# Paired logits in one PSUM tile and a second top-p search cut into eight steps

## The chip, the cores and the metric

The kernel runs on one core of one Trainium2 chip. The metric is the device time of one execution in microseconds (us), lower is better. The engines of the core work side by side and each takes its instructions in program order: TensorE (PE, matmuls and transposes; its weight loads are PEld in the profile), VectorE (DVE), ScalarE (ACT), GpSimd (POOL) and the DMA queue of SyncE (SP). Matmul results land in PSUM, whose tiles are handed out from pools with a fixed number of buffers.

## The reference, cut to what matters

The network has four layers over 3327 nodes with 256 features. The change touches the last layer only. It does two steps of a diffusion by a given matrix `S` and of an attention whose weights are cut to the most probable 90% of each row:

```python
def _top_p_attention(X, W1, W2, W3):
    q = X @ W1.T @ W2.T
    k = X @ W3.T
    logits = q @ k.T / TAU
    probs = jax.nn.softmax(logits, axis=-1)
    idx = jnp.argsort(-probs, axis=-1)
    sp = jnp.take_along_axis(probs, idx, axis=-1)
    cs = jnp.cumsum(sp, axis=-1)
    keep_sorted = cs - sp < TOP_P                 # TOP_P = 0.9
    mask = ...                                    # the kept places of each row
    A = probs * mask
    return A / jnp.maximum(A.sum(-1, keepdims=True), 1e-12)

R = (S + I) / row sums
Xf = Xa = X
for n in range(2):
    A = _top_p_attention(Xa, W1, W2, W3)
    Xf = R @ Xf                                   # diffusion
    Xa = A @ Xa                                   # attention
    Z = Z + Xf @ U1[n].T + Xa @ U2[n].T
h = X + Z                                         # then layer norms
```

`W1` to `W3` have 64 rows, so a logit is a product over 64 numbers. All arithmetic is fp32.

## The kernel before

The nodes are padded to 3328, which makes 26 tiles of 128 rows (`nt = 26`, `npad = 3328`). A tile of logits `e` is 128 x 3328. Queries and keys lie twice on the partitions, at 0 to 63 and at 64 to 127, so the left and the right half of a row of logits come from two matmuls over 64 partitions each (`half = 1664`, in chunks of `KC = 416`):

```python
def scores(work, psum, p, q, e):
    for c0 in range(0, half, KC):
        for h in (0, DA):                          # DA = 64
            c = c0 + (half if h else 0)
            w = min(KC, n - c)
            pl = psum.tile([P, 512], F32, name="sc")          # two buffers
            nc.tensor.matmul(pl[:, :w], q[h:h + DA, :], kT[p][h:h + DA, c0:c0 + w], start=True, stop=True)
            nc.scalar.copy(e[:, c:c + w], pl[:, :w])
        yield
```

The diffusion of a tile is 26 matmuls of 128x256 (`diffused`, line L721 in the profile). The attention of a tile transposes `e` in 26 blocks of 128x128 through PSUM tiles of four blocks each, ACT copies them to SBUF, and 26 matmuls follow (`attended`, lines L749, L751 and L753; two PSUM buffers `tp`, three SBUF buffers `wt`).

The first attention finds the threshold of a row with `search_short` (Exp on ACT, 26 Max8 over segments of 128 columns, six rounds of Max8 and MatchReplace, and one pass that keeps what lies above). The second has flatter rows and takes `search_long`, which guesses a threshold twice before it ranks the candidates:

```python
def search_long(work, sm, e, total, v, kept):
    nc.vector.max(m8, e[:, :KC])                                            # L815
    ...
    nc.scalar.activation(junk, e, AF.Exp, ..., accum_out=root)              # L819
    nc.scalar.activation(e, e, AF.Exp, bias=neg, accum_out=total)           # L820
    yield
    ...                                                                     # c1 from total and root
    nc.scalar.activation(junk, e, AF.Sign, bias=c1, scale=-1.0, accum_out=sg)                  # L829
    z = work.tile([P, npad], F32, name="z", bufs=1)
    nc.vector.scalar_tensor_tensor(z, e, c1, e, op0=ALU.is_ge, op1=ALU.mult, accum_out=m1)     # L831
    nc.vector.tensor_scalar(k1, sg, -0.5, npad / 2, op0=ALU.mult, op1=ALU.add)
    ...                                                                     # c2 from k1, m1
    nc.scalar.activation(junk, e, AF.Relu, bias=nc2, accum_out=f2)          # L849
    nc.scalar.activation(junk, e, AF.Sign, bias=c2, scale=-1.0, accum_out=sg)                  # L850
    ...
    yield
    nc.vector.tensor_scalar(k2, sg, -0.5, npad / 2, op0=ALU.mult, op1=ALU.add)                 # L863
    ...                                                                     # c3 from k2, f2
    nc.vector.scalar_tensor_tensor(z, e, c3, e, op0=ALU.is_lt, op1=ALU.mult, accum_out=rest)   # L875
    cand = segment_tops(work, z)                                            # 26 Max8, L761
    top = ranked(work, cand, RPT)                                           # L770, L772
    cs = crossing(work, v, top, base, lim)
    ...                                                                     # ties
    for r, c in ((r, half), (up, 0)):
        ...
        nc.vector.match_replace(back, drop, back, 0.0)                      # L894
    nc.vector.scalar_tensor_tensor(e, e, v, e, op0=ALU.is_ge, op1=ALU.mult, accum_out=kept)    # L895
    yield
```

Both attentions run in one loop over tiles, which works on several tiles at once so that the engines have something to do; a scheduler orders the instructions of each engine when the program is built:

```python
with ... tc.tile_pool(name="l3p", bufs=2, space=PSUM) as psum:
    for p, search, step, lead in ((0, search_short, first, (1,)), (1, search_long, second, (2, 1, 0))):
        for i in range(-lead[0], nt):
            # scores of tile i + lead[0], diffusion of a tile up to DL = 4 ahead,
            # one step of the search of each tile in lead, then:
            todo = step(work, psum, i, attended(work, psum, es[i], G if p else X), f, xfs[i])
```

`first` multiplies the result of the first attention with `U1` and `U2` and makes the keys and queries of the second (lines L913 to L929); `second` adds up and applies the layer norms (L936 to L952). `e` has three buffers, `sc`, `acc`, `tp` and `pj` two each.

Of the kernel before, what the change touches and what calls it, by code (L numbers as in the profile page):

```python
# [9 lines left out]
F32 = mybir.dt.float32  # L10
# [28 lines left out]
DL = 4  # L39
# [4 lines left out]
def gnn_kernel(ctx: ExitStack, tc: tile.TileContext, n: int, a: dict, out: bass.AP):  # L44
# [441 lines left out]
    with tc.tile_pool(name="l3", bufs=1) as pool, tc.tile_pool(name="l3d", bufs=1, space=DRAM) as dram:  # L486
# [213 lines left out]
        def scores(work, psum, p, q, e):  # L700

            if npad > n:
                nc.gpsimd.memset(e[:, n:], NEG)
            for c0 in range(0, half, KC):
                for h in (0, DA):
                    c = c0 + (half if h else 0)
                    w = min(KC, n - c)
                    pl = psum.tile([P, 512], F32, name="sc")
                    nc.tensor.matmul(pl[:, :w], q[h:h + DA, :], kT[p][h:h + DA, c0:c0 + w], start=True, stop=True)  # L709
                    nc.scalar.copy(e[:, c:c + w], pl[:, :w])  # L710
                yield
# [30 lines left out]
        def attended(work, psum, e, rhs):  # L742

            acc = psum.tile([P, D], F32, name="acc")
            for j0 in range(0, nt, 4):
                m = min(4, nt - j0)
                pt = psum.tile([P, 4, P], F32, name="tp")
# [7 lines left out]
            return acc  # L755

        def segment_tops(work, z):

            cand = work.tile([P, nseg * 8], F32, name="cand")
            for s in range(nseg):  # L760
                nc.vector.max(cand[:, s * 8:(s + 1) * 8], z[:, s * SEG:(s + 1) * SEG])  # L761
            return cand
# [30 lines left out]
        def search_short(work, sm, e, total, v, kept):  # L793


            top = ranked(work, segment_tops(work, e), RP0)
# [8 lines left out]
        def search_long(work, sm, e, total, v, kept):  # L805
# [22 lines left out]
            sg, k1, m1 = t("sg"), t("k1"), t("m1")  # L828
            nc.scalar.activation(junk, e, AF.Sign, bias=c1, scale=-1.0, accum_out=sg)  # L829
            z = work.tile([P, npad], F32, name="z", bufs=1)  # L830
            nc.vector.scalar_tensor_tensor(z, e, c1, e, op0=ALU.is_ge, op1=ALU.mult, accum_out=m1)  # L831
            nc.vector.tensor_scalar(k1, sg, -0.5, npad / 2, op0=ALU.mult, op1=ALU.add)
            rc, na = t("rc"), t("na")
# [12 lines left out]

            nc2, f2, k2, m2 = t("nc2"), t("fs2"), t("k2"), t("m2")
            nc.vector.tensor_scalar_mul(nc2, c2, -1.0)
            nc.scalar.activation(junk, e, AF.Relu, bias=nc2, accum_out=f2)  # L849
            nc.scalar.activation(junk, e, AF.Sign, bias=c2, scale=-1.0, accum_out=sg)  # L850
# [27 lines left out]
            cand = segment_tops(work, z)  # L878
            top = ranked(work, cand, RPT)
            cs = crossing(work, v, top, base, lim)  # L880

# [7 lines left out]
            for r, c in ((r, half), (up, 0)):  # L889
# [3 lines left out]
                back = e[:, c:c + half][:, ::-1]  # L893
                nc.vector.match_replace(back, drop, back, 0.0)  # L894
            nc.vector.scalar_tensor_tensor(e, e, v, e, op0=ALU.is_ge, op1=ALU.mult, accum_out=kept)  # L895
# [9 lines left out]
        def first(work, psum, it, acc, f, xf):  # L905
# [9 lines left out]
            nc.vector.tensor_copy(xt, pt)  # L915
            ps = psum.tile([P, 2, D], F32, name="pj")
            pg = psum.tile([P, 2, D], F32, name="pj")
            for k in range(4):
                nc.tensor.matmul(ps[:, 0, :], xt[:, k, :], (u1 if k < 2 else u2)[:, 0, k % 2, :],  # L919
                                 start=(k == 0), stop=(k == 3))  # L920
# [12 lines left out]
        def second(work, psum, it, acc, f, xf):  # L933
# [3 lines left out]
            yield  # L937
# [5 lines left out]
            power(rs, mv)  # L943
            nc.vector.scalar_tensor_tensor(h, h, mv[:, 0:1], g3, op0=ALU.subtract, op1=ALU.mult)
# [4 lines left out]
            power(rs, mv)  # L949
            nb = small.tile([P, 1], F32, name="nb")  # L950
# [6 lines left out]
        def unresolved(sm, psum, p):  # L957
# [14 lines left out]
            pf = psum.tile([1, nt], F32, name="pj")  # L972
# [12 lines left out]
        with tc.tile_pool(name="l3w", bufs=2) as work, tc.tile_pool(name="l3s", bufs=4) as sm, \  # L985
                tc.tile_pool(name="l3at", bufs=3) as atp, tc.tile_pool(name="l3p", bufs=2, space=PSUM) as psum:


            for p, search, step, lead in ((0, search_short, first, (1,)), (1, search_long, second, (2, 1, 0))):
                es, searches, xfs, todo = {}, {}, [], None  # L990
                for i in range(-lead[0], nt):
# [11 lines left out]
                    if p:  # L1003
                        for x in parts:
                            both(x)
# [159 lines left out]
```

## Time and profile before

| what | value |
|---|---|
| time, median of 3 (lowest, highest) | 3961.54 us (3959.18, 3976.78) |
| span of the profiled execution | 3960.8 us |
| busy: PE, DVE, ACT, POOL | 3568.0, 2724.9, 1677.1, 367.0 us |
| layers before the last one | 0 to about 2039 us |
| first attention | about 2039 to 2996 us |
| second attention | about 2996 to 3961 us |

An fp32 matmul appears as two records. The records of matmuls that follow each other overlap, so the cost of a group of them is read from where it starts to where the next one starts. In the timeline, `[0.59 <-ACT e L710]` means that the engine stood idle for 0.59 us before this group and that an ACT instruction of line L710 ended the wait. A bare `issue` is idle time for which the profile shows no wait.

### The profile page before, as it was taken

What the parts mean: (1) busy time and instruction counts of PE and PEld (TensorE: products, weight loads), DVE (VectorE), ACT (ScalarE), POOL (GpSimd) and SP (SyncE); (2) the same over time, 40 slices, a digit from 0 to 9 for tenths busy, and PEclk for the clock granted to TensorE, in tenths of its full rate; (3) what the DMA queues carried; (4) which work ended last, traced back from release to release, by engine and by line L of the source; (5) the groups of instructions that cost most, each with busy time, mean ns of one, the idle gap of its engine ahead of it and who ended that gap; (6) DMA issues with size and microseconds to landing.
All of it is one profiled execution on the core that took longest, in us unless ns stands there. A gap on an engine that the chain in (4) does not pass through costs nothing.

```text
span 3960.8 us, 41368 instructions
## 1 busy us (share of the span) xinstructions
PE 3568.0 (90%) x14863; PEld 2605.8 (66%) x14863; DVE 2724.9 (69%) x6003; ACT 1677.1 (42%) x2692; POOL 367.0 (9%) x436
## 2 busy tenths in 40 slices
PE   9999988888888877789989999999999899999975
PEld 8888754444444433378877777777777677777754
DVE  1111589999999999967743444444453999999996
ACT  0000555455555556311112333333345666666662
POOL 0000000101010101011110000000000122222210
PEclk9999999999999988889999999999999999999997
DMA  6442211111111000044422121112103122222100
GB/s 234 140 138 91 76 46 41 35 36 34 41 35 35 23 0 0 15 140 151 145 87 81 48 60 58 51 52 60 58 11 102 48 59 62 62 61 61 48 23 6
DMA packets 100530, 252.95 MB, mean 64 GB/s; under 512 B 14787, under 2 KB 49091, under 8 KB 100179
## 3 DMA queue, kind: packets, MB, share of 16 engines
q1 hardware_dynamic: 100306, 250.13, 20.7%
q8 instruction: 121, 1.98, 0.2%
q14 instruction: 103, 0.84, 0.1%
HBM read 239.86 MB, written 10.22 MB: 63 GB/s over the span
## 4 chain that ended last, share of the span: by engine, by line
PE 34%; DVE 16%; ACT 3%; issue 2%; POOL 2%; DMA 0%; POOLq 0%; ACTq 0%; DVEq 0%
PE acc L753 12%; PE acc L721 8%; PE acc L651 6%; PE sc L709 3%; DVE cand L761 3%; DVE e L894 2%; DVE e L895 2%; PE tp L749 2%; PE pj L919 1%; DVE top L770 1%; DVE z L831 1%; DVE z L875 1%; ACT junk L829 1%; DVE rest L772 1%; POOL rs L513 1%
## 5 line engine op out<-in xcount | busy, mean ns | idle before, releaser
L464 PE MATMUL y<-h,ident 128*128 128x512 f32 (+1 forms) x896 | 445.3, 644 | 72.6 <-DVE h L411 72.4
L408 DVE TENSOR_TENSOR_SCAN h<-dA,carry,db 128x512 f32<-128x512 f32 (+1 forms) x448 | 510.3, 1189 | 0.1
L761 DVE MAX8 cand<-e 128x8 f32<-128x128 f32 x676 | 143.8, 279 | 478.1 <-ACT e L710 478.1
L753 PE MATMUL acc<-G,wt 128*128 128x256 f32 x1352 | 344.3, 409 | 47.1 <-ACT wt L751 47.1
L464 PEld LDWEIGHTS y<-h,ident 128*128 128x128 f32 x896 | 188.5, 218 | 291.1 <-issue 179.6
L751 ACT COPY wt<-tp 128x512 f32<-128x512 f32 (+1 forms) x364 | 186.1, 552 | 443.0 <-PE tp L749 442.6
L753 PEld LDWEIGHTS acc<-G,wt 128*128 128x128 f32 x1352 | 269.7, 204 | 120.0 <-ACT wt L751 80.7
L239 PE MATMUL cb<-F,at 128*128 128x256 f32 x1352 | 334.0, 393 | 8.3 <-ACT m L256 8.2
L710 ACT COPY e<-sc 128x416 f32<-128x416 f32 (+1 forms) x416 | 192.5, 508 | 329.0 <-PE sc L709 329.0
L721 PE MATMUL acc<-X,at 128*128 128x256 f32 x1352 | 321.5, 388 | 2.6 <-issue 2.6
L753 PE MATMUL acc<-X,wt 128*128 128x256 f32 x1352 | 318.9, 383 | 3.0 <-ACT wt L751 2.8
L239 PEld LDWEIGHTS cb<-F,at 128*128 128x128 f32 x1352 | 261.3, 196 | 89.5 <-issue 33.5
L116 PE MATMUL acc<-xa,at 128*128 128x257 f32 x1352 | 308.4, 382 | 5.9 <-DMA at<-in_adjT 5.9
L721 PE MATMUL acc<-F,at 128*128 128x256 f32 x1352 | 308.6, 380 | 0.0
L651 PE MATMUL acc<-F,at 128*128 128x257 f32 x1352 | 303.9, 381 | 1.1 <-DVE at L648 1.1
L721 PEld LDWEIGHTS acc<-X,at 128*128 128x128 f32 x1352 | 251.7, 192 | 75.8 <-issue 44.1
L753 PEld LDWEIGHTS acc<-X,wt 128*128 128x128 f32 x1352 | 250.1, 190 | 64.2 <-ACT wt L751 33.5
L393 ACT ACTIVATE dA<-dt,A_log 128x512 f32<-128x512 f32 (+1 forms) x448 | 281.0, 681 | 12.6 <-DVE dt L370 12.2
L709 PE MATMUL sc<-kT,q 64*128 64x416 f32 x832 | 259.9, 561 | 27.5 <-ACT e L710 26.6
L116 PEld LDWEIGHTS acc<-xa,at 128*128 128x128 f32 x1352 | 255.9, 191 | 42.8 <-issue 5.9
L721 PEld LDWEIGHTS acc<-F,at 128*128 128x128 f32 x1352 | 249.6, 189 | 46.5 <-issue 13.7
L651 PEld LDWEIGHTS acc<-F,at 128*128 128x128 f32 x1352 | 253.7, 191 | 36.8 <-DVE at L648 1.4
(293 smaller groups left out, 5292.2 us busy)
## 6 DMA issues: line engine op xcount, KB each, us to landing
at<-in_adjT SPq DMA_DIRECT2D x102, 832.0 KB, 4.5
at<-in_adjT SPq DMA_DIRECT2D x156, 448.0 KB, 3.4
at<-in_adjT SPq DMA_DIRECT2D x52, 576.0 KB, 3.7
at<-in_adjT SPq DMA_DIRECT2D x52, 320.0 KB, 3.0
at<-in_adjT SPq DMA_DIRECT2D x26, 512.0 KB, 3.5
xt<-in_xT SPq DMA_DIRECT2D x26, 128.0 KB, 4.1
qd<-q SPq DMA_DIRECT2D x104, 32.0 KB, 1.9
q<-qd SPq DMA_DIRECT2D x52, 64.0 KB, 1.9
```

Source lines behind the costliest of these rows:

```text
L116: nc.tensor.matmul(acc, at[:, j, :], rhs[:, j0 + j, :], start=(j0 + j == 0), stop=(j0 + j == nt - 1))
L239: nc.tensor.matmul(acc, at[:, j % JC, :], X0[:, j, :], start=(j == 0), stop=(j == nt - 1))
L393: nc.scalar.activation(dA[:, g, :], dt[:, g, :], AF.Exp, scale=A[:, g, s:s + 1])
L408: nc.vector.tensor_tensor_scan(h[:, g, :], dA[:, g, :], db[g // 2][:, g % 2, :], initial=carry[:, s, g:g + 1], op0=ALU.mult, op1=ALU.add)
L464: nc.tensor.matmul(ys[g][:, :w], ident, h[:, g, :], start=False, stop=(s == DS - 1))
L651: nc.tensor.matmul(acc, at[:, j, :], F[:, j0 + j, :], start=(j0 + j == 0), stop=(j0 + j == nt - 1))
L709: nc.tensor.matmul(pl[:, :w], q[h:h + DA, :], kT[p][h:h + DA, c0:c0 + w], start=True, stop=True)
L710: nc.scalar.copy(e[:, c:c + w], pl[:, :w])
L721: nc.tensor.matmul(acc, at[:, j, :], rhs[:, j0 + j, :], start=(j0 + j == 0), stop=(j0 + j == nt - 1))
L751: nc.scalar.copy(wt[:, :m, :], pt[:, :m, :])
L753: nc.tensor.matmul(acc, wt[:, j, :], rhs[:, j0 + j, :], start=(j0 + j == 0), stop=(j0 + j == nt - 1))
L761: nc.vector.max(cand[:, s * 8:(s + 1) * 8], z[:, s * SEG:(s + 1) * SEG])
```

## The change

It does five things.

1. The two products of a pair of logits write the two halves of one PSUM tile of two banks, which has one buffer. The two matmuls are given priority, so that the scheduler puts them next to each other, and one ACT copy takes both; the last pair of a tile has unequal halves (416 and 415 columns) and keeps two copies.
2. In the second search the masked pass of DVE that summed what lies above the first guess (L831 before) becomes a Relu pass of ACT with an accumulator; one more small DVE instruction makes the sum from it.
3. The second search gets eight places to stop in place of three, and the loop of the second attention is written out: the attention of a tile is taken one round later, in pieces between the steps of two searches.
4. The second attention gets its own PSUM pool, in which `tp` has four buffers.
5. For the last tile alone the final pass is cut into two halves. `first` and `second` also get one or two more places to stop.

It is meant to take work from DVE, to keep TensorE from waiting between the two halves of a pair, and to let transposes run ahead of ACT.

```diff
-                for h in (0, DA):
-                    c = c0 + (half if h else 0)
-                    w = min(KC, n - c)
-                    pl = psum.tile([P, 512], F32, name="sc")
-                    nc.tensor.matmul(pl[:, :w], q[h:h + DA, :], kT[p][h:h + DA, c0:c0 + w], start=True, stop=True)
-                    nc.scalar.copy(e[:, c:c + w], pl[:, :w])
+                pl = psum.tile([P, 2, 512], F32, name="sc", bufs=1)
+                ws = [min(KC, n - c0 - h * half) for h in range(2)]
+
+                with tc.high_priority():
+                    for h, w in enumerate(ws):
+                        k = slice(h * DA, (h + 1) * DA)
+                        nc.tensor.matmul(pl[:, h, :w], q[k, :], kT[p][k, c0:c0 + w], start=True, stop=True)
+                if ws[0] == ws[1]:
+                    nc.scalar.copy(halves[:, :, c0:c0 + ws[0]], pl[:, :, :ws[0]])
+                else:
+                    for h, w in enumerate(ws):
+                        nc.scalar.copy(halves[:, h, c0:c0 + w], pl[:, h, :w])
 ...
-                pt = psum.tile([P, 4, P], F32, name="tp")
+                pt = psum.tile([P, 4, P], F32, name="tp", bufs=tp)
 ...
-            sg, k1, m1 = t("sg"), t("k1"), t("m1")
+            nc1, f1, sg, k1, m1 = t("nc1"), t("fs1"), t("sg"), t("k1"), t("m1")
+            nc.vector.tensor_scalar_mul(nc1, c1, -1.0)
+            nc.scalar.activation(junk, e, AF.Relu, bias=nc1, accum_out=f1)
+            yield
             nc.scalar.activation(junk, e, AF.Sign, bias=c1, scale=-1.0, accum_out=sg)
-            z = work.tile([P, npad], F32, name="z", bufs=1)
-            nc.vector.scalar_tensor_tensor(z, e, c1, e, op0=ALU.is_ge, op1=ALU.mult, accum_out=m1)
+            yield
             nc.vector.tensor_scalar(k1, sg, -0.5, npad / 2, op0=ALU.mult, op1=ALU.add)
+            nc.vector.scalar_tensor_tensor(m1, k1, c1, f1, op0=ALU.mult, op1=ALU.add)
 ...
             nc.scalar.activation(junk, e, AF.Relu, bias=nc2, accum_out=f2)
+            yield
             nc.scalar.activation(junk, e, AF.Sign, bias=c2, scale=-1.0, accum_out=sg)
 ...
-            cand = segment_tops(work, z)
+            cand = candidates(work)
+            segment_tops(cand, z, 0, nseg // 2)
+            yield
+            segment_tops(cand, z, nseg // 2)
             top = ranked(work, cand, RPT)
             cs = crossing(work, v, top, base, lim)
+            yield
 ...
+                part = e[:, c:c + half]
+                nc.vector.match_replace(part[:, ::-1], drop, part[:, ::-1], 0.0)
+                if halves:
+                    nc.vector.scalar_tensor_tensor(part, part, v, part, op0=ALU.is_ge, op1=ALU.mult,
+                                                   accum_out=sums[:, i:i + 1])
 ...
             nc.vector.tensor_copy(xt, pt)              # in first()
+            yield
 ...
+            with tc.tile_pool(name="l3q", bufs=2, space=PSUM) as psum:
+                for i in range(-2, nt + 1):
+                    if 0 < i:
+                        values = attended(work, psum, es[i - 1], G, tp=4)
+                    weigh(2)                           # so many groups of four blocks
+                    search(i)
+                    search(i + 1)
+                    weigh(2)
+                    search(i + 1)
+                    weigh(3)
+                    search(i)
+                    ...                                # second() of tile i - 1 begins
+                    logits = start(1, i + 2, es, searches, search_long) if i + 2 < nt else iter(())
+                    spread = diffused(work, atp, psum, 1, more[0], xfs) if more else iter(())
+                    next(logits, None)
+                    next(logits, None)
+                    next(spread, None)
+                    search(i + 1)
+                    both(logits)
+                    next(spread, None)
+                    search(i + 1)
+                    search(i + 2)
+                    next(result, None)
+                    both(spread)
+                    search(i)
+                    ...
```

## The prediction

> **What bounds the kernel now.** Only the last layer changes, so I first read busy times by stretch: a steady stretch of the first attention (20 tiles) and one of the second (18 tiles). The columns are start and end, length, then busy time (and instructions) of PE, PEld, DVE, ACT and POOL, granted clock, DMA share, GB/s.
>
> ```profile
> 2143.50:2869.10 725.60, 709.24 (x3401) 551.37 (x3400) 318.81 (x1081) 247.05 (x461) 20.42 (x40) 1.00 0.19 55
> 3144.20:3760.10 615.90, 571.54 (x2626) 442.75 (x2625) 584.14 (x2036) 415.56 (x468) 139.94 (x144) 0.98 0.21 60
> ```
>
> The first attention is bound by PE: 709.2 of 725.6 us busy, 36.3 us a tile, DVE at 44%. The second is bound by DVE: 584.1 of 615.9 us (95%), at 34.2 us a tile, with PE close behind at 93% and ACT at 67%. So the two stretches must be asked separately.
>
> PE's busy time contains waits. In the timeline of PE I look at the logits (L709), first in the first attention, then in the second:
>
> ```profile
> 2516.09 0.96 PE L709 MATMUL sc<-kT,q 64*128 64x416 f32 x2
> 2516.98 3.72 PE L753 MATMUL acc<-X,wt 128*128 128x256 f32 x16
> ...
> 2530.16 0.97 PE L709 MATMUL sc<-kT,q 64*128 64x416 f32 x4
> 2531.06 3.29 PE L721 MATMUL acc<-X,at 128*128 128x256 f32 x14
> ```
>
> ```profile
> 3410.38 0.97 PE L709 MATMUL sc<-kT,q 64*128 64x416 f32 x4
> 3411.93 1.37 PE L709 MATMUL sc<-kT,q 64*128 64x416 f32 x4 [0.59 <-ACT e L710]
> 3413.49 1.37 PE L709 MATMUL sc<-kT,q 64*128 64x416 f32 x4 [0.19 <-ACT e L710]
> 3414.79 10.22 PE L721 MATMUL acc<-F,at 128*128 128x256 f32 x46
> ...
> 3430.57 1.04 PE L749 MATMUL tp<-ident,e 128*128 128x128 f32 x8
> 3431.54 0.96 PE L709 MATMUL sc<-kT,q 64*128 64x416 f32 x2
> 3432.43 3.72 PE L753 MATMUL acc<-G,wt 128*128 128x256 f32 x16
> ```
>
> From start to the next start, a single half (two records) costs 0.89 us and so does a pair whose halves stand together (four records): the halves run at the same time. A pair that waits for ACT to empty a buffer costs 1.55. Two singles cost twice what a pair costs.
>
> **What the Trainium skill says.** "TensorE: Matmul & The Clock Gate", Part 3: Packing small matmuls, says that matmuls on different row groups run concurrently; the 0.89 us for one half and for two agree. "TensorEngine Tiling (Array Packing)", Gotcha 1: PSUM Pressure, wants different row tiles in different PSUM banks; the new tile gives each half its own 2 KB, and before they were two tiles. "Perfetto Trace Analysis", Optimizing Scalar/DVE Operations, advises to move work to ScalarE when DVE is saturated; the saturation is in the table above. Its section Identifying the Most-Contended Engine picks the bound by occupancy. That would promise the whole of what DVE loses here, and I depart from it below.
>
> **Part 1, pairs, in the first attention.** In a steady tile two singles and three pairs stand in PE's order; in the changed program's order all four pairs stand together, with at least three matmuls (1.3 us) between pairs, enough for one copy. (A copy of 416 columns takes 0.51 us and ACT streams 3328 in 3.07, so 832 should take 0.51 + 0.38 = 0.89.) Saved: 2 x 0.89 - 0.89 = 0.89 us a tile on the bounding engine, for some 23 tiles: 20 us. Also, PE waits for the copy `xt` in each tile (16.2 us in these 20 tiles, in the groups by line); the new order puts eight transposes and four attention matmuls ahead of what needs it. Half of that wait should come back as a wait for the first `wt` after those transposes: 0.4 x 22 = 8 us saved. Together 28 us.
>
> **Part 2, the second attention by occupancy.** DVE loses L831, 3.68 us plus 0.08 for the read of its accumulator, and gains two instructions of about 0.1: 32.45 (584.1 / 18) - 3.6 = 28.8 us a tile. ACT gains a pass, 3.07 + 0.19, and saves 0.13 on each of three copies: 23.1 + 2.9 = 26.0. PE: L721 costs 10.06 / 46 = 0.219 a record, L753 3.56 / 16 = 0.223, a transpose 0.97 / 8 = 0.121; 52 x 0.219 + 52 x 0.223 + 26 x 0.121 + 4 x 0.89 = 29.7. PE would become the bound at some 30 us and 26 tiles would gain about 100 us.
>
> **Part 3, what stands against it: the round trip.** DVE is in order, and in the changed program's order of DVE I follow one turn from `nc2` (the input of the second guess) to the next `nc2`. Of three successive tiles two have, between `nc2` and the instruction that reads the Sign pass on `c2`, only the layer-norm steps of an older tile, about 2.9 us of DVE work. The masking pass, the 26 Max8 and the ranking, which covered these ACT passes before, now stand on either side of them. ACT has to run Relu, one copy of logits and Sign in that time. Their durations from the timeline:
>
> ```profile
> 3433.34 0.14 DVE L848 TENSOR_SCALAR nc<-c 128x1 f32<-128x1 f32 x1
> ...
> 3433.51 3.07 ACT L849 ACTIVATE junk<-e,nc 128x3328 bf16<-128x3328 f32 x1 [1.23 <-DVE nc L848]
> ...
> 3436.71 3.07 ACT L850 ACTIVATE junk<-e,c 128x3328 bf16<-128x3328 f32 x1
> ```
>
> 0.17 + 3.2 + 0.8 + 3.2 = 7.4 us. The rest of the turn is in the last tile, where DVE runs it alone:
>
> ```profile
> 3903.18 3.68 DVE L875 SCALAR_TENSOR_TENSOR z<-e,c 128x3328 f32<-128x3328 f32 x1
> ...
> 3912.21 0.38 DVE L770 MAX8 top<-cand 128x8 f32<-128x208 f32 x1
> ...
> 3917.04 0.32 DVE L779 TENSOR_TENSOR_SCAN cs<-ones,base,top 128x48 f32<-128x48 f32 x1
> ...
> 3919.45 1.88 DVE L894 MATCH_REPLACE8 e<-drop,e 128x1664 f32<-128x1664 f32 x1
> ...
> 3923.49 3.68 DVE L895 SCALAR_TENSOR_TENSOR e<-e,v 128x3328 f32<-128x3328 f32 x1
> ```
>
> Mask and 26 Max8: 9.0; with the five small steps of the next tile between them, 9.4. Ranking 4.8, with `xf` 5.2. Crossing and ties 2.4. Two MatchReplace 3.7. Final pass 3.6. Small dependent steps, at the 0.13 to 0.2 us by which they follow each other: nine to `c3` 1.6, nine from `k1` 1.2, nine to `nc2` and the Max8 of the next tile 1.4. Sum: 7.4 + 1.6 + 9.4 + 5.2 + 2.4 + 3.7 + 1.2 + 3.6 + 1.4 = 35.9 us. In every third tile `nc2` comes early, and MatchReplace and the final pass cover most of the ACT passes. For this tile and the one before it the same sum gives about 67, with the Sign pass still ending some 0.5 us after DVE is ready. Three tiles: 102.9, or 34.3 us a tile, where it was 34.2. So the 3.7 us taken from DVE come back as idle time of DVE behind ACT. The estimate is good to about 1 us a tile, 25 us in all; since serial sums of small steps tend to be too long, I take a gain of 0.2 a tile, 5 us.
>
> **Part 4, ends.** The order puts the logits of the first three tiles into the first 30 us of the second attention, where the second tile's came 34 us after the first's; its head should lose PE's idle 8.3 us there, minus the longer search: 5 us. The last tile's first half is ready 1.8 us earlier, and four transpose groups run ahead: 3 us. The new PSUM pool must wait for the old one: 2 us lost. Transposes in advance and saved PE time in the steady second attention are off the path.
>
> Sum: 28 + 5 + 5 + 3 - 2 = 39 us; 3961 - 39 = 3922.
>
> **The rivals.** (a) Occupancy decides: the round trip is hidden by some freedom I miss, PE sets 30 to 31.5 us a tile, and the time is 3840 to 3880. For it: PE at 93% and DVE at 95% were both dense before. Against it: DVE's order is fixed and nothing else stands between those two instructions. (b) ACT becomes what all wait for: six passes of 3.26 us a tile, with `wt` copies queued behind them, stall PE in the attention as well, and the turn takes 35.5 us or more: 3950 to 3970. For it: L753 already waits for ACT 30.4 us in these 18 tiles. Against it: four `tp` buffers, and PE has 4 us a tile to spare if DVE sets the pace. (c) The pair's single buffer makes PE wait for each copy in the first attention: the 28 us shrink to 10, and the time is about 3940.
>
> **Range and chances.** (b) and (c) together bound the high end, a half success of (a) the low end: 3875 to 3958. Faster by over 2% needs less than 3882, more than half of (a): 0.14. Slower by over 2% needs 3 us a tile lost: 0.02. The rest, 0.84.
>
> **What would show it.** Right: a first attention of about 35 us a tile with no single halves; a second one still at 33.5 to 34.5 us, DVE busy down to about 29 us a tile, with a new wait of DVE for the Sign pass on `c2` of 3 to 4.5 us in two of three tiles, and ACT waiting for `nc2`. Wrong: if that wait is under 1 us and PE is above 96% in the second attention, then (a) holds and Part 3 failed; if PE waits for `wt` by more than 3 us a tile, (b); if PE waits for `sc` in the first attention, (c).

## The result and the profile after

| | before | after |
|---|---|---|
| time, median (range), us | 3963.49 (3959.18 to 3976.78) | 3917.91 (3908.57 to 3928.28) |
| ratio to before, 95% interval | | 0.988 [0.984, 0.992] |
| first attention, us a tile | 36.27 | 34.65 |
| second attention, steady, us a turn | 34.22 | 34.97 |
| DVE busy and idle in such a turn, us | 32.45 and 1.76 | 30.40 and 4.57 |

A turn is the time from one `nc2` to the next, as in the prediction; it is the mean of 18 turns from the fifth `nc2` on, and the busy time is the union of DVE's records. The layers that the change doesn't touch end 11.5 us apart in the two profiled runs (first logits at 2044.0 before and at 2055.5 after), so below stretches of the last layer are compared and not whole spans.

From the first logits to the end the layer took 1916.7 us and now takes 1871.0, 45.7 less. The ledger, from the start of the first logits, the end of the last weighted sum of the first attention and the starts of `nc2` in the two traces:

| stretch | before | after | difference |
|---|---|---|---|
| first logits to the last weighted sum of the first attention | 945.4 | 906.5 | -38.9 |
| from there to the fifth `nc2` of the second attention | 169.4 | 174.1 | +4.7 |
| 18 steady turns | 615.9 | 629.4 | +13.5 |
| from there to the end | 186.0 | 161.0 | -25.0 |

The busy times by stretch of the changed kernel, first 20 tiles of the first attention, then the 18 turns (start and end, length, PE, PEld, DVE, ACT, POOL, granted clock, DMA share, GB/s):

```profile
2178.43:2871.33 692.90, 687.38 (x3401) 544.62 (x3399) 325.12 (x1081) 243.77 (x401) 20.41 (x40) 1.00 0.20 58
3136.08:3765.52 629.44, 575.66 (x2631) 443.71 (x2630) 547.12 (x2034) 462.13 (x450) 76.75 (x144) 0.95 0.19 59
```

The first attention is still bound by PE (99%). In the second no engine is dense any more: PE 91%, DVE 87%, ACT 73%. The work that left DVE went to ACT as meant, and the turn grew all the same.

The timeline of PE in the first attention of the changed kernel:

```profile
2498.83 0.38 PE L943 MATMUL pj<-ident,xf 128*128 128x128 f32 x2
2499.05 0.38 PE L943 MATMUL pj<-ident,xa 128*128 128x128 f32 x2
2499.27 1.04 PE L756 MATMUL tp<-ident,e 128*128 128x128 f32 x8
2500.54 1.99 PE L760 MATMUL acc<-X,wt 128*128 128x256 f32 x8 [0.24 <-ACT wt L758]
2502.37 1.89 PE L950 MATMUL pj<-U,xt 128*128 128x256 f32 x8
...
2509.96 0.97 PE L712 MATMUL sc<-kT,q 64*128 64x416 f32 x4
2510.86 1.56 PE L760 MATMUL acc<-X,wt 128*128 128x256 f32 x6
2512.35 0.97 PE L712 MATMUL sc<-kT,q 64*128 64x416 f32 x4
```

Every pair (L712) stands together as four records and costs 0.90 us to the next start; none waits for its single buffer, since three matmuls (six records, 1.5 us) lie between pairs, or one matmul and five transposes (1.2 us). The transposes of `xf` and `xa` are followed by eight transposes and four attention matmuls (eight records), and `xt` is no longer waited for; a small wait for `wt` has come in its place.

The gap from `nc2` to `k2` in the second attention, DVE and ACT from the timeline:

```profile
3277.38 0.15 DVE L866 TENSOR_SCALAR nc<-c 128x1 f32<-128x1 f32 x1
...
3277.57 3.07 ACT L867 ACTIVATE junk<-e,nc 128x3328 bf16<-128x3328 f32 x1
...
3280.60 0.48 DVE L969 SCALAR_TENSOR_TENSOR h<-acc,f,xf 128x256 f32<-128x256 f32 x1 [2.61 <-PE acc L760]
3280.64 0.83 ACT L714 COPY e<-sc 128x832 f32<-128x832 f32 x1
...
3281.37 3.07 ACT L869 ACTIVATE junk<-e,c 128x3328 bf16<-128x3328 f32 x1
...
3283.05 0.48 DVE L978 SCALAR_TENSOR_TENSOR h<-h,rs,t 128x256 f32<-128x256 f32 x1 [0.77 <-POOL rs L513]
...
3285.28 0.16 DVE L985 SCALAR_TENSOR_TENSOR nb<-mv,rs 128x1 f32<-128x1 f32 x1 [1.07 <-POOL rs L513]
3285.36 0.15 DVE L882 TENSOR_SCALAR k<-sg 128x1 f32<-128x1 f32 x1
```

Relu, copy and Sign follow each other on ACT as in the prediction, and `k2` comes 8.0 us after `nc2`. But no wait for Sign is shown. DVE's idle time is spread over the layer-norm steps of the older tile, which wait for PE's attention and twice for GpSimd, and `k2` comes 0.84 us after the end of the read of Sign's accumulator (3284.53). Over the 18 turns `k2` comes 0.03 to 0.84 us after it: two paths of nearly the same length end the gap. What DVE waited for in the 18 turns (in total, times, longest):

```profile
DVE h L969 <- PE acc L760: 27.7, 12, 2.6
DVE nb L985 <- POOL rs L513: 16.9, 18, 1.1
DVE h L978 <- POOL rs L513: 10.7, 18, 0.8
DVE m L830 <- ACT e L714: 9.5, 6, 2.3
DVE k L882 <- ACT junk L869: 0.8, 1, 0.8
```

In the 18 turns before the change the two longest were these (L863 is `k2`):

```profile
DVE nb L951 <- POOL rs L513: 13.6, 9, 2.1
DVE k L863 <- ACT junk L850: 7.7, 8, 1.3
```

DVE was idle between `nc2` and `k2` for 0.68 us a turn then, and is for 2.97 now.

The lengths of the turns repeat in threes, 35.8, 27.7 and 40.5 to 42.3 us. In the first two the gap holds layer-norm steps only and DVE is idle in it for 4.3 and 4.7 us; in the third it holds MatchReplace and final pass and DVE is not idle in it.

At the end of the last tile the two halves of the final pass:

```profile
3891.01 1.88 DVE L918 MATCH_REPLACE8 e<-drop,e 128x1664 f32<-128x1664 f32 x1
3892.80 1.94 DVE L920 SCALAR_TENSOR_TENSOR e<-e,v 128x1664 f32<-128x1664 f32 x1
...
3894.67 1.95 DVE L920 SCALAR_TENSOR_TENSOR e<-e,v 128x1664 f32<-128x1664 f32 x1
```

### The profile page after: what moved, and what is told of

It reads as the page before. It is cut to its first block, busy times and chain, and to the rows that moved or that the text cites. A ratio compares the mean times of both kernels' runs of the same rounds, so it can differ in the third digit from the quotient of the medians.

```text
span 3926.5 us, 41305 instructions
## 1 busy us (share of the span) xinstructions
PE 3541.6 (90%) x14863; PEld 2592.1 (66%) x14863; DVE 2670.0 (68%) x6006; ACT 1739.0 (44%) x2588; POOL 301.0 (8%) x436
## 5 line engine op out<-in xcount | busy, mean ns | idle before, releaser
L760 PE MATMUL acc<-G,wt 128*128 128x256 f32 x1352 | 359.5, 424 | 75.9 <-ACT wt L758 74.6
L760 PEld LDWEIGHTS acc<-G,wt 128*128 128x128 f32 x1352 | 279.8, 213 | 154.0 <-ACT wt L758 88.2
L760 PE MATMUL acc<-X,wt 128*128 128x256 f32 x1352 | 343.9, 391 | 10.0 <-ACT wt L758 9.5
L728 PE MATMUL acc<-X,at 128*128 128x256 f32 x1352 | 308.8, 383 | 2.8 <-issue 2.8
L116 PEld LDWEIGHTS acc<-xa,at 128*128 128x128 f32 x1352 | 256.4, 191 | 42.3 <-issue 5.5
L405 DVE TENSOR_TENSOR db<-du,row 128x1024 f32<-128x1024 f32 (+1 forms) x224 | 250.8, 1136 | 35.6 <-ACT row L390 35.1
L411 DVE TENSOR_TENSOR h<-h,C 128x2048 f32<-128x2048 f32 (+1 forms) x112 | 238.2, 2127 | 31.5 <-PE C L401 26.7
```

The source lines that it names most:

```text
L116: nc.tensor.matmul(acc, at[:, j, :], rhs[:, j0 + j, :], start=(j0 + j == 0), stop=(j0 + j == nt - 1))
L405: nc.vector.tensor_mul(db[i], du[:, 2 * i:2 * i + 2, :], B.to_broadcast([P, 2, w]))
L411: nc.vector.tensor_mul(h, h, C.to_broadcast([P, NG, w]))
L728: nc.tensor.matmul(acc, at[:, j, :], rhs[:, j0 + j, :], start=(j0 + j == 0), stop=(j0 + j == nt - 1))
L760: nc.tensor.matmul(acc, wt[:, j, :], rhs[:, j0 + j, :], start=(j0 + j == 0), stop=(j0 + j == nt - 1))
```

## The experiments

Each is told by its edit against the changed kernel, unless another is named. "First" is the stretch from the first logits to the last weighted sum of the first attention (945.4 us before, 906.5 changed), "second" the rest (971.3 and 964.5). The table gives the steady turn, DVE's busy and idle time in it, and the part of the idle time that lies between `nc2` and `k2`. The kernels ran on several chips, each beside the kernel before, whose median was 3963.5 to 3974.1 us; so small differences are read from the ratios and the stretches.

| kernel | median, us | ratio to before, 95% | first | second | turn | DVE busy | idle | in the gap |
|---|---|---|---|---|---|---|---|---|
| before | 3963.5 | | 945.4 | 971.3 | 34.22 | 32.45 | 1.76 | 0.68 |
| changed | 3917.9 | 0.988 [0.984, 0.992] | 906.5 | 964.5 | 34.97 | 30.40 | 4.57 | 2.97 |
| extra ACT pass | 3940.3 | 0.993 [0.991, 0.995] | 906.6 | 981.8 | 35.69 | 30.48 | 5.22 | 3.55 |
| masking pass on DVE | 3916.8 | 0.987 [0.986, 0.989] | 906.6 | 952.8 | 34.74 | 32.95 | 1.79 | 0.48 |
| gap filled | 3970.8 | 1.002 [1.001, 1.003] | 906.5 | 1015.7 | 37.54 | 30.22 | 7.32 | 0.00 |
| gap half filled | 3939.5 | 0.994 [0.993, 0.995] | 904.9 | 981.5 | 36.15 | 30.75 | 5.40 | 2.76 |
| gap filled, early `c1` | 3891.9 | 0.982 [0.980, 0.984] | 906.5 | 933.1 | 33.64 | 31.24 | 2.40 | 0.00 |
| the same, two pair buffers | 3913.0 | 0.985 [0.983, 0.987] | 904.9 | 952.0 | 34.21 | 31.19 | 3.02 | 0.07 |
| gap filled, early `c1`, old first loop | 3880.9 | 0.978 [0.975, 0.980] | 898.2 | 932.2 | 33.60 | 31.21 | 2.40 | 0.00 |
| the same, single halves in the second | 3908.5 | 0.984 [0.982, 0.986] | 898.2 | 958.0 | 33.97 | 30.07 | 3.90 | 0.22 |
| before, with pairs | 3935.0 | 0.992 [0.991, 0.994] | 896.7 | 990.2 | 35.85 | 32.24 | 3.61 | 1.65 |
| changed, without pairs | 4032.1 | 1.017 [1.015, 1.019] | 1022.4 | 955.1 | 34.17 | 30.26 | 3.91 | 2.36 |
| changed first, old second | 3970.0 | 1.001 [1.000, 1.002] | 904.9 | 1013.2 | 36.34 | 32.65 | 3.69 | 0.24 |
| the same, two pair buffers | 3961.1 | 0.999 [0.998, 1.000] | 904.9 | 1002.5 | 35.84 | 32.58 | 3.27 | 0.90 |

The theory was Part 3 of the prediction: DVE idles behind ACT between `nc2` and `k2`, which takes back what Part 2 took from it. The rival: ACT's copies of weights, queued behind its long passes, and PE's waits for them set the turn.

**Masking pass on DVE again.**

```diff
-            nc.vector.tensor_scalar_mul(nc1, c1, -1.0)
-            nc.scalar.activation(junk, e, AF.Relu, bias=nc1, accum_out=f1)
+            z = work.tile([P, npad], F32, name="z", bufs=1)
+            nc.vector.scalar_tensor_tensor(z, e, c1, e, op0=ALU.is_ge, op1=ALU.mult, accum_out=m1)
             yield
             nc.scalar.activation(junk, e, AF.Sign, bias=c1, scale=-1.0, accum_out=sg)
...
-            nc.vector.scalar_tensor_tensor(m1, k1, c1, f1, op0=ALU.mult, op1=ALU.add)
```

> The changed kernel, with the mass above the first guess summed by the masking pass on DVE again, as in the kernel before, and no Relu on the first guess: DVE 3.6 us a tile more, ACT 3.26 less; all else as changed. The order on DVE moves with it: in nearly every tile the MatchReplace and the final pass stand between nc2 and k2. My theory: the gap is covered (31.5 us) and the pass is added (3.7): 35 us a tile, the time within 15 us of the changed kernel: 3900 to 3930. Rival, ACT and PE's waits for weights set the pace: with 3.26 us a tile less on ACT the tile falls to 32 to 33 us and the time to 3840 to 3865.

Measured: 3916.8 us, the time of the changed kernel. The 18 turns:

```profile
3122.34:3747.73 625.39, 566.97 (x2631) 433.27 (x2630) 593.18 (x2049) 411.48 (x416) 97.09 (x144) 0.96 0.21 59
```

DVE is at 95% again, as it was before the change, and its idle time in the gap falls from 2.97 to 0.48 us. So the move of this pass to ACT, taken by itself inside the new order, is worth nothing: busy time turned into idle time, 2.55 us of one for 2.78 of the other. With 2.8 us a turn less on ACT (411.5 against 462.1 us in 18 turns) the turn didn't fall to 32 or 33 us, so the rival found no support. This run doesn't separate the two cleanly, as DVE's 32.95 us leave no turn below 33. In the traces the second attention is 11.7 us shorter with the masking pass: the start up to the fifth `nc2` 15.7 and the 18 turns 4.0 us shorter, the end 8.0 longer. So the move to ACT gained nothing, and may have lost a little.

**One ACT pass more in the gap.**

```diff
+            nc.scalar.activation(junk[:, :832], e[:, :832], AF.Sign, bias=c2, scale=-1.0)
             nc.scalar.activation(junk, e, AF.Sign, bias=c2, scale=-1.0, accum_out=sg)
```

> The changed kernel with one useless ACT pass more: Sign over 832 columns (about 0.85 us by the copy of that size) between the Relu and the Sign of the second guess, written where the next pass writes. DVE's order stays as it was. Theory of Part 3, the gap from nc2 to k2 is ended by ACT: each turn whose gap holds only layer-norm steps, two of three, is 0.8 us longer, and the third too where MatchReplace and the final pass end before Sign: 13 to 20 us, 3931 to 3938. Rival, the gap is ended by the layer-norm chain, which came 0.9 us after Sign's end in the trace: it has 0.9 us to spare and the time stays within 5 us of 3918. A plain occupancy view (ACT busy 73%) also says no change.

Measured: 3940.3 us, 2 above the range; the second attention 17.3 us longer, 0.72 us a turn, where 13 to 20 were expected. The same place in its timeline, ACT and the end of the gap:

```profile
3281.38 0.15 DVE L866 TENSOR_SCALAR nc<-c 128x1 f32<-128x1 f32 x1
...
3285.37 0.99 ACT L869 ACTIVATE junk<-e,c 128x832 bf16<-128x832 f32 x1
...
3286.39 3.07 ACT L870 ACTIVATE junk<-e,c 128x3328 bf16<-128x3328 f32 x1
...
3289.58 0.15 DVE L883 TENSOR_SCALAR k<-sg 128x1 f32<-128x1 f32 x1 [0.23 <-ACT junk L870]
```

`k2` now comes 0.03 us after Sign's read in all 18 turns, and the wait is named as the prediction named it. The pass took 0.99 us, of which the layer-norm chain's lead hid a part. Both rivals fell: the layer-norm chain, which would have held the time within 5 us, and the occupancy view, by which an engine at 73% has room for the pass. PE's wait for weights grew with it, from 51.2 to 64.3 us in 18 turns, so this run alone doesn't rule out that ACT acts on the turn through PE. Below, a change of DVE's order alone moves the turn by 3.9 us.

**The gap filled.** The order on DVE can be pinned: what stands in `issue_after(x)` is issued behind `x`, without a wait for its end.

```diff
-                nc.vector.match_replace(part[:, ::-1], drop, part[:, ::-1], 0.0)
+                with behind(t_ + 1):     # issue_after(nc2 of the next tile), where there is one
+                    nc.vector.match_replace(part[:, ::-1], drop, part[:, ::-1], 0.0)
...
-                nc.vector.scalar_tensor_tensor(e, e, v, e, op0=ALU.is_ge, op1=ALU.mult, accum_out=kept)
+                with behind(t_ + 1):
+                    nc.vector.scalar_tensor_tensor(e, e, v, e, op0=ALU.is_ge, op1=ALU.mult, accum_out=kept)
```

> The changed kernel with one difference in order: in the second attention both MatchReplace and the final pass of each tile are issued on DVE behind nc2 of the next tile, in every tile and not only in every third. Same instructions, same work. My theory (the turn is the round trip nc2, Relu, copy, Sign, k2, on which DVE stands idle): the 7.3 us of MatchReplace and final pass now lie inside the gap of 7.4 to 8.0 us, the layer-norm steps (2.9 us) come out of it; the sum of Part 3 becomes 7.4 + 1.6 + 9.4 + 2.9 + 5.2 + 2.4 + 1.2 + 1.4 = 31.5 us a tile, with up to 1 us more for the wait at k1, against the 35.2 us of the changed kernel: 60 to 85 us off, 3830 to 3860. Rival, ACT's copies of weights behind its long passes and PE's waits for them set the pace: these instructions are the same, the tile stays at 34 to 35.5 us and the time at 3890 to 3920.

Measured: 3970.8 us, 53 more than the changed kernel where 60 to 85 less were expected. The gap was filled as meant: 7.66 us, no idle time, in each of 18 turns. DVE and ACT, and PE's weighted sum, one gap earlier in the same turn:

```profile
3413.69 0.14 DVE L846 TENSOR_SCALAR nc<-c 128x1 f32<-128x1 f32 x1
...
3413.92 3.07 ACT L847 ACTIVATE junk<-e,nc 128x3328 bf16<-128x3328 f32 x1 [3.29 <-DVE rc L854]
...
3417.12 3.07 ACT L849 ACTIVATE junk<-e,c 128x3328 bf16<-128x3328 f32 x1
...
3420.19 1.54 ACT L759 COPY wt<-tp 128x512 f32<-128x512 f32 x3
3420.31 0.15 DVE L851 TENSOR_SCALAR k<-sg 128x1 f32<-128x1 f32 x1 [3.56 <-ACT junk L849]
...
3420.80 10.09 PE L761 MATMUL acc<-G,wt 128*128 128x256 f32 x32 [4.66 <-ACT wt L759]
```

The change has two round trips of a Relu and a Sign pass, not one: `nc1` to `k1` takes 6.6 us as well. In the changed order Max8, ranking and crossing, and in two of three turns MatchReplace, covered that one. Taken away from there to fill the other gap, they left DVE idle at `k1` for 3.56 us a turn; ACT in turn idles 3.29 us, because `nc1` is issued among the last rounds of the ranking though its Exp passes ended at 3410.6. The sum of Part 3 has no term for this round trip. The trace of the changed kernel already showed its start: ACT waits for `nc1` in 12 of the 18 turns, 26.0 us in all.

**Half of it.** As above, with the final pass alone behind `nc2`.

```diff
-                with behind(t_ + 1):
-                    nc.vector.match_replace(part[:, ::-1], drop, part[:, ::-1], 0.0)
+                nc.vector.match_replace(part[:, ::-1], drop, part[:, ::-1], 0.0)
```

> As the kernel with the filled gap, but only the final pass (3.7 us) is issued behind nc2 of the next tile; both MatchReplace stay ahead of nc2. My theory: the gap of 7.4 us or more is half covered, the layer-norm steps have left it, so the sum is 7.4 + 1.6 + 9.4 + 2.9 + 5.2 + 2.4 + 3.7 + 1.2 + 1.4 = 35.2 us a tile, what the changed kernel takes: 3900 to 3925. Were the regular order or the earlier layer norm what counts, and not the covered gap, it would gain as much as the filled one.

Measured: 3939.5 us, 14 above the range. Ranking, crossing and MatchReplace cover `k1` (wait 0.18 us), and 2.76 us of the other gap stay open: better than the filled gap, worse than the changed kernel.

**The gap filled and the first guess formed early.** Added to the filled gap:

```diff
             for r in range(rounds):
+                # from the third round on: issue_after(nc1 of the next tile)
                 nc.vector.max(top[:, r * 8:(r + 1) * 8], left)
```

> The kernel with MatchReplace and final pass behind nc2, and in addition rounds three to six of the ranking issued behind nc1 of the next tile, so that the first guess c1 is formed as soon as its two Exp passes are done and not after the ranking. Revised theory: a turn is a loop through ACT (six passes and the copies between, 26 us busy) and the DVE steps which form the next bias; with the gap at nc2 filled, the loop is held up at nc1, 3.3 us a turn, and at k1, 3.6 us. Then the early c1 takes 2.5 to 3.3 us off each turn of 37.5: 34.2 to 35 us a tile, 60 to 70 us off 3971, 3900 to 3915. Rival, DVE's and ACT's waits follow from PE, whose weights wait behind the passes: the turn stays within 1 us of 37.5, 3945 to 3975.

Measured: 3891.9 us, 79 less than the filled gap and 8 below the range. The turn is 33.64 us, 3.9 less, where 2.5 to 3.3 were expected. The rival, by which the turn stays within 1 us, fell. The same places:

```profile
3405.62 0.15 DVE L847 TENSOR_SCALAR nc<-c 128x1 f32<-128x1 f32 x1
...
3405.87 3.07 ACT L848 ACTIVATE junk<-e,nc 128x3328 bf16<-128x3328 f32 x1 [0.73 <-DVE nc L847]
...
3412.26 0.15 DVE L852 TENSOR_SCALAR k<-sg 128x1 f32<-128x1 f32 x1 [0.33 <-ACT junk L850]
...
3412.75 8.86 PE L761 MATMUL acc<-G,wt 128*128 128x256 f32 x32 [2.11 <-ACT wt L759]
```

Relu starts 0.73 us after Exp's read, the rest of the ranking covers Relu and Sign, and both waits at once are nearly gone. No instruction was added or removed: 79 us lay in the place of four small ones. DVE's idle time is 2.40 us a turn. PE's wait for weights fell with the turn, from 4.7 to 2.3 us. An early `c1` without the filled gap was not run, so the two shares aren't separated.

**More PSUM for the logits.** To the last kernel: `sc` with two buffers in the second attention, `tp` with two in place of four.

```diff
-                pl = psum.tile([P, 2, 512], F32, name="sc", bufs=1)
+                pl = psum.tile([P, 2, 512], F32, name="sc", bufs=nb)      # nb = 2 in the second
...
-                        values = attended(work, psum, es[i - 1], G, tp=4)
+                        values = attended(work, psum, es[i - 1], G, tp=2)
```

> The best kernel so far (3892) with the four PSUM banks given otherwise in the second attention: two buffers for the pair of logits, two for the transposes instead of four. Theory of the loop through ACT (33.7 us a turn, of which ACT is busy 26 and waits 4.7 us for the next pair, one after another, while PE does six other matmuls between pairs): with two pair buffers half or more of that wait goes, 2 to 3 us a turn, until DVE at 31 us a turn becomes the bound: 3830 to 3860. Rival, the transposes ahead of ACT's long passes are what the PSUM is worth: with two buffers PE waits longer for weights, the turn stays or grows: 3890 to 3930.

Measured: 3913.0 us, in the rival's range, but not for its reason: PE waits for weights 2.2 us a turn, about what it waited with one pair buffer (2.3). ACT's waits between 3120 and 3720 us, with one pair buffer and four for transposes:

```profile
ACT e L715 <- PE sc L713: 56.1, 36, 1.6
ACT e L718 <- PE sc L713: 27.7, 18, 1.5
```

and with two and two:

```profile
ACT wt L759 <- PE tp L757: 99.9, 35, 3.7
...
ACT e L715 <- PE sc L713: 18.2, 17, 1.1
```

The Trainium skill, "Perfetto Trace Analysis", Optimization Strategy, says that a bubble which repeats can mean too little PSUM for the next tile. Here the bubble did repeat in every turn, on ACT, and the second buffer cut it from 83.8 to 18.2 us. But two buffers of the transposes were given up for it, and ACT now waits 99.9 us for transposes, where it was 5.1.

**The best of both.** The kernel with early `c1`, and the first attention's loop and projection as before the change (pairs kept):

```diff
-                        values = attended(work, psum, es[i], X)
-                        next(values)
-                        if todo is not None:
-                            next(todo)
-                        todo = first(work, psum, i, last_of(values), f, xfs[i])
+                        acc = last_of(attended(work, psum, es[i], X))
+                        todo = first(work, psum, i, acc, f, xfs[i])
                         next(todo)
```

> The best kernel so far (MatchReplace and final pass behind nc2, early c1; 3892) with the first attention's loop and projection of the kernel before, logits in pairs. In the run with pairs alone that loop took 826.0 us from the first to the last weighted sum of X, where the changed loop takes 834.2 in every run. If these stretches add up: 8 us less, 3884. Rival, the second attention's head depends on how the first one ends, and gives it back: 3890 to 3895.

Measured: 3880.9 us, ratio 0.978 [0.975, 0.980] to before. The stretches add up: the first attention takes what it took with pairs alone (898.2 and 896.7 us), the second what it took with early `c1` (932.2 and 933.1). It beats both kernels.

**Single halves in its second attention.** `single_scores` is `scores` of the kernel before; all else as in the best:

```diff
-                return scores(work, psum, p, q, es[t])
+                return (single_scores if p else scores)(work, psum, p, q, es[t])
```

> The best kernel so far (3881) with single halves of logits (two buffers of one bank, one copy each) in the second attention alone; the four buffers for the transposes stay. ACT's logits copies cost 4 x 0.15 us a tile more, PE's halves stand together or not as the order has it. Theory of the loop through ACT: what it loses by waiting 4.7 us a turn for the next pair falls by half or more with two halves in flight, and here no transpose buffer is given up for it: 31.5 to 32.5 us a turn, 3835 to 3860. Rival: what the loop loses there it loses at another wait (weights behind ACT's passes, DVE at 31 us a turn), as when the pair had two buffers: 3875 to 3915.

Measured: 3908.5 us, in the rival's range again: ACT's wait for logits fell from 4.7 to 2.1 us a turn, and PE now waits 1.9 us a turn for their buffers. But the steady turn grew by only 0.37 us, 6.6 in 18 turns. Of the 25.8 us that the second attention lost, 21.7 lie before the fifth `nc2`; neither theory spoke of that stretch, and why it grew stays open.

**Pairs alone, in the kernel before.** Its `scores` is replaced by the new one, nothing else:

```diff
-                    pl = psum.tile([P, 512], F32, name="sc")
-                    nc.tensor.matmul(pl[:, :w], q[h:h + DA, :], kT[p][h:h + DA, c0:c0 + w], start=True, stop=True)
-                    nc.scalar.copy(e[:, c:c + w], pl[:, :w])
+                pl = psum.tile([P, 2, 512], F32, name="sc", bufs=1)
... # and the rest of the new scores
```

> The kernel before with only the logits changed: pairs in one PSUM tile of two banks (one buffer), one copy, in both attentions; loops, pools and searches as before. My theory (a pair costs PE what a single half costs, and the first attention is bound by PE): the first attention loses 0.89 us a tile, about 20 us in all. In the second attention with the old loop, where four pairs follow each other, PE waits for each copy (as it did with the pairs on this loop before), so that this attention gives 20 to 40 us back: 3955 to 3985 in all. Rival, pairs are harmless there and what was lost with the old loop came from elsewhere: 3935 to 3945.

Measured: 3935.0 us. The sum is the rival's, but not its halves. The first attention lost 48.7 us where 20 were expected, and the second gave back 18.9, just under the 20 to 40. Its reason was another than the expected one: PE never waits long enough for the pair's buffer to be listed, but 3.5 us a turn for weights (1.6 before). PE in its first attention:

```profile
2530.01 0.38 PE L920 MATMUL pj<-ident,xa 128*128 128x128 f32 x2
2530.23 1.04 PE L756 MATMUL tp<-ident,e 128*128 128x128 f32 x8
2531.18 1.99 PE L926 MATMUL pj<-U,xt 128*128 128x256 f32 x8
```

With pairs the scheduler puts eight transposes ahead of the projection by itself, so that nothing waits for `xt`, nor for `wt`. A tile takes 34.27 us, 2.00 less than before and 0.38 less than in the changed loop.

**The changed kernel without pairs.** The same diff read backwards, in the changed kernel.

> The changed kernel with the logits as before: single halves in two buffers, one copy each; the loops, the search and the pools as changed. My theory: the first attention is 0.89 us a tile longer on PE (about 20 us of the 37 us that the change gained there come back, the rest stays with the order of the layer's projection); the second attention is not bound by PE and ACT is 0.4 us a tile busier, so it is up to 10 us longer: 3935 to 3950. Rival, the pairs bring all of the first attention's 37 us: 3950 to 3965.

Measured: 4032.1 us, 82 above the range and 67 above the rival's. The first attention is 116 us longer. One timeline of it, PE and ACT:

```profile
2513.53 1.04 PE L749 MATMUL tp<-ident,e 128*128 128x128 f32 x8
2514.19 3.07 ACT L807 ACTIVATE e<-e,neg 128x3328 f32<-128x3328 f32 x1 [2.34 <-DVE neg L806]
...
2517.26 1.05 ACT L751 COPY wt<-tp 128x512 f32<-128x512 f32 x2
...
2517.87 2.53 PE L753 MATMUL acc<-X,wt 128*128 128x256 f32 x8 [3.30 <-ACT wt L751]
```

Exp starts 1.1 us after PE starts the transposes of `xf`, where in the changed kernel it starts 12.4 us ahead of them, and the copy of the first weights is queued behind it. PE waited 63.2 us so in 19 places between 2156 and 2882 us. In the first attention the new loop needs the pairs; the pairs don't need the new loop. The second attention went against both theories: it is 9.4 us shorter without pairs, its turn 34.17 us and not 34.97.

**The changed first attention with the old second one.** Three-step search, masking pass on DVE, two `tp` buffers, the old loop; pairs kept:

```diff
-                        values = attended(work, psum, es[i - 1], G, tp=4)
...
+                    for x in parts:                       # logits, then diffusion
+                        both(x)
+                    if todo is not None:
+                        next(todo)
+                    for part in (2, 1, 0):
+                        if 0 <= i + part < nt:
+                            next(searches[i + part])
```

> The first attention as changed, the second with the search in three steps, the masking pass on DVE, two tp buffers and the loop of the kernel before; logits in pairs in both. My theory: the first attention keeps its 37 us, the second steps at 34.2 us a tile as before, 1 us less than as changed, but loses what the new head gained: 3915 to 3925, the same as the changed kernel within 10 us. Rival, the steps of the second attention cost the changed kernel as much as the traces' 1 us a tile say: 3890 to 3900.

Measured: 3970.0 us. Both theories missed: the old second attention with pairs takes 36.34 us a turn and not 34.22. PE waits there 57.0 us for the pair's buffer between 3120 and 3720 us, 3.6 a turn.

**The same with two pair buffers.**

```diff
-                pl = psum.tile([P, 2, 512], F32, name="sc", bufs=1)
+                pl = psum.tile([P, 2, 512], F32, name="sc", bufs=nb)      # nb = 2 in the second
```

> The changed first attention with the old loop and search in the second, as tried before, but with two buffers for the pair in the second attention (four banks). Theory, the single buffer makes PE wait for each copy (3.6 us a tile) and this delays the next logits: the second attention falls back to 34.2 us a tile and the time to 3915 to 3935. Rival, the order of the old loop with pairs is at fault and not the buffer: it stays at 3955 to 3975.

Measured: 3961.1 us; the rival held. The wait for the buffer is gone from PE's list, and the turn still takes 35.84 us. PE's waits for weights are 68.5 us in the same stretch, where they were 28.4 in the kernel before. Why the old order has more of them with pairs stays open; no run isolates it.

## Why the prediction was right, and where it was not

3922 was predicted and 3918 measured. That closeness is in part luck: the first attention and the ends gained 25.2 us more than predicted, and the steady turns of the second, which were to gain 5, lost 13.5.

- **Part 1.** The mechanism held. The 0.89 us a tile for the pairs measured 0.89 (from start to next start, logits cost PE 89.6 us in the 20 tiles that the prediction read, and 71.9 in 20 tiles after). The wait for `xt` went wholly, 0.81 us a tile, and 0.27 came back as the wait for `wt` (5.3 us in 20 tiles), a third, where half was assumed. 34.65 against 36.27 is 1.62 a tile where 1.29 was taken; 0.2 of it is in neither term and stays unassigned. The stretch lost 38.9 us where 28 were taken. What failed is the credit: the order of the changed loop is not needed for the `xt` term. The pairs alone bring it, and the new loop costs 8 us against them (834.2 and 826.0 us from the first to the last weighted sum).
- **Part 2.** ACT's 26.0 us a turn measured 25.67. DVE's 28.8 measured 30.40: passes over 1 us fell by 3.5 us a turn, but steps under 0.24 us cover 5.34 us of the union where it was 3.96. There are three more of them a turn, and they stand in rows, where earlier they overlapped longer instructions. That occupancy would not decide was right: DVE and PE are both below 92%.
- **Part 3.** The turn in two parts, 35.9 and 67 us, measured 35.8 and 68 to 70; three turns 102.9 and 104.9. The missing 0.7 us a turn lies mostly in the third kind of turn, where DVE waits for the first logits (L830, 2.3 us at most) and for GpSimd. The gap of 7.4 us measured 7.6, 8.0 and 8.7, and DVE's idle time in it 4.3 and 4.7 us in two of three turns, as predicted. The wait was named wrongly: the sign that the prediction gave, a wait for Sign of 3 to 4.5 us in two of three tiles, shows as 0.8 us in all. In these two kinds of turn `k2` mostly follows the layer-norm steps, 0.47 or 0.84 us after Sign's read, and only with one more ACT pass did Sign end the gap everywhere. The theory behind the part, that filling this gap would pay, fell in its first test: the step left out was the other round trip, `nc1` to `k1`. With both covered the turn fell to 33.6 us.
- **Part 4.** Mis-sized in both directions. The stretch up to the fifth `nc2` grew by 4.7 us instead of falling by 5, for a reason that stays open; the end from the last steady turn on fell by 25.0 instead of 3. After the last `nc2` the kernel before still ran 26 Max8 and the ranking of the tile before the last; the changed order has only MatchReplace and the final pass left there (83.1 and 68.7 us from that `nc2` to the end). The other 10.6 us lie in the three turns before it, 102.9 us before and 92.2 now.
- **The sum.** -28 measured -38.9; -5 measured +13.5 in the steady turns; the ends, -6, measured -20.3. Together -45.7 for -39.
- **The rivals.** (a) didn't come. (b) is half there: PE waits for `wt` 51.2 us in 18 turns, 2.8 a turn, where it was 1.6, close to the 3 that were named as its sign, but taking 2.8 us a turn off ACT, with DVE back at 95%, changed nothing. (c) didn't come in the first attention. With the old second loop it came in one kernel (changed first, old second: 3.6 us a turn) and not in another (pairs alone).

## What to carry to other kernels

Work moved to another engine can come back as a round trip, as here: look at what the first engine has to do, in its own order, between the bias it sends and the result it reads, for every such pair, before counting the saved pass. Cover was a fixed stock here: filling one gap emptied another until small producers were issued earlier, and with the gap filled the place of four small instructions was worth 79 us, more than the whole change. Try the parts of a change alone: in the first attention the pairs were worth 48.7 us with the old loop and 115.9 with the new one.

## What the runs showed of the hardware

The granted clock of PE in the steady second attention was 0.98 before, 0.95 changed, 0.91 with the gap filled and 0.96 with `c1` early, where PE stood idle for 2.4, 3.0, 4.7 and 2.3 us a turn. The sum of the waits alone doesn't set it: with the extra ACT pass 4.0 us go with 0.95, with pairs alone 3.5 us with 0.93. What the traces show is where the clock is lost. After a wait of 4.66 us 32 records of the weighted sum took 10.09 us, at a granted clock of 0.71 in that stretch; after 2.11 us they took 8.86, at 0.81; 16 records without a wait before them took 3.72, at 1.00. The Trainium skill, "TensorE: Matmul & The Clock Gate", Part 1: The HAM clock gate, says that the clock is throttled unless PE is kept active; the direction agrees. Against twice 3.72 us these waits cost 2.65 and 1.42 us more than their length, which no term of the prediction had.

A Sign pass over 832 columns without an accumulator took 0.99 us, where the copy of the same width out of PSUM took 0.83 to 0.88.
